# A graph attention layer on one core: Wo's tiles in PSUM, two low halves on another engine, and three steps issued sooner

## The chip, the core and the metric

The kernel runs on one core of a Trainium2 chip. A core has a matrix engine (TensorE, PE in the profile, with its weight loads as PEld), three engines that work on tiles (VectorE is DVE, ScalarE is ACT, GpSimd is POOL), and a queue that issues transfers (SyncE, SP). Each runs its own list of instructions in order; semaphores make one wait for another. Tiles lie in SBUF; TensorE adds its products up in PSUM, which this kernel uses as banks of 128 x 512 float32.

The metric is the device time of one launch, in microseconds (us). Lower is better. All times below without a unit are in us.

## What is computed

A layer norm with ReLU in front, graph attention with 16 heads of 64 and two projections one behind the other for q, k and v, and a residual sum. N is 384 rows, D is 1024 columns.

```python
h = jnp.maximum(_layernorm(x, axis=-1), 0.0)
q = h @ wq.T + bq
k = h @ wk.T + bk
v = h @ wv.T + bv
q2 = (q @ wiq.T + biq).reshape(N, H, D).transpose(1, 0, 2)
k2 = (k @ wik.T + bik).reshape(N, H, D).transpose(1, 0, 2)
v2 = (v @ wiv.T + biv).reshape(N, H, D).transpose(1, 0, 2)
mask = _build_mask(edge_index, edge_type, edge_type_weights, x.dtype)
scores = jnp.einsum('hnd,hmd->hnm', q2, k2) * scale + mask[None]
attn = jax.nn.softmax(scores, axis=-1)
out = jnp.einsum('hnm,hmd->hnd', attn, v2)
out = out.transpose(1, 0, 2).reshape(N, OUT_F)
x = x + out @ wo.T + bo
```

The mask is built from 6,528 edges: softplus of an edge type's weight where there is an edge, minus infinity elsewhere.

## The kernel before

**Weights.** Seven matrices of 1024 x 1024 are read in eight pieces (chunks) of 128 x 1024 float32, 512 KB each, in one sequence of 56: eight of Wv (0 to 7), Wq (8 to 15), Wiv (16 to 23) and Wk (24 to 31), then Wiq and Wik by turns (32 to 47: 33, 35, 37 are Wik's first, second and third), then Wo (48 to 55). `load(w)` issues the transfer of chunk w on SP's queue into one of four buffers `raw`.

**Two halves.** Every product is made from three: high x high, high x low and low x high (`mm3`, lines 494 to 496). Each chunk is therefore split. `split_hi` has ScalarE write the high half (line 102, float16 with a scale; line 108 for Wik, without one). The low half is what is left: `split_lo` (lines 125 and 127) in one instruction, `lo_half` (118) in two parts on VectorE, `lo_pieces` (113) in four parts on GpSimd.

**Slots.** Chunks 0 to 31 are taken one at a time, a slot each. `slot_head(w)` first splits chunk w + 2, finishes the products of the slot before (`flush`), sums up what the summing loads brought (`scan_sum`), then issues `load(w + 5)` and `scan_load(w)`. TensorE's 24 matmuls of the slot follow, or 18 with 512 columns for Wiv.

**Summing loads.** The weights Wiv, Wk, Wiq, Wik and Wo are read a second time, ahead of their use, for a bound on their rows that sets the float16 scale (`SCANS`, `scan_load`, line 146). ScalarE squares or takes absolute values and sums (line 155), or VectorE reduces (line 153). When all eight pieces of a matrix are there, `bound_max` (line 182) reduces them, TensorE transposes the result (line 187, `bound`), and VectorE makes scales of it (lines 162 to 201).

**Mask and residual.** GpSimd scatters the edges into a table in memory (line 351), issues three mask loads from it (360), and adds the bias bo to x in six pieces of 128 x 512 (`residual_add`, line 666) in slots 26 to 31. VectorE merges the three mask loads into the mask, a copy under a condition each (`mask_select`, line 364), in the heads of chunks 33 to 35, and scales it (744).

**Attention.** From chunk 32 on a hand-written schedule of 60 steps runs. At even steps below 48, `do_S` makes two tiles of scores (line 957, PSUM banks of tag "s", four of them). VectorE adds the mask and takes the minimum (966), ScalarE takes the exponential (971) and writes the high half of the normalised row block (1001), VectorE the low half (1005), and SP transposes both by a transfer (1009); the last two tiles go through TensorE, ScalarE and VectorE (1014, 1020, 1021). Eight attention products (`av_mm`, line 1029) follow, at steps 14, 20, 26, 32, 38, 44, 50 and 54; each is evacuated by ScalarE (1034) and split by VectorE and GpSimd (1037, 1038).

**Filling.** Between these TensorE works off a list. `fill(n)` hands out as many units as a step has left: `STEP` less what the scores and the attention product take, divided by `UNIT`. First come the products of chunks 32 to 47 (`fill_qk`, bank tag "g", three of them), whose heads (`qk_head`) hold the splits and loads for later chunks, then those of Wo (`fill_o`). A product of Wo, `omm(t, h, k)`, is three matmuls of 512 columns for one of six output tiles and one of eight chunks. All six tiles are added up in two groups: chunks 0 to 3, then a sum into the result (`ysum`, line 902), then chunks 4 to 7 in a new bank and another sum. `wo_prep` splits Wo's chunk 2 to 7 at the steps in `WSTEPS`; `wready` holds the step from which a chunk may be used. Behind the loop stand the products with the last chunk, each with its sum and its transfer to memory; the sixth tile is done in two halves of 256 columns.

`later` is a list that is worked off in the next step, behind its line 966; what is put there by an entry of it runs a step later still.

Of the kernel before, what the change touches and what calls it, by code (L numbers as in the profile page):

```python
# [19 lines left out]
N, D, NT, KT, NP = 384, 1024, 3, 8, 8  # L20
# [7 lines left out]
def gnn_kernel(ctx: ExitStack, tc: tile.TileContext, x, edges, erows, etw, wq, wk, wv, wiq, wik, wiv, wo,  # L28
# [6 lines left out]
    nc = tc.nc  # L35
# [497 lines left out]
    w = 0  # L533
# [8 lines left out]
    def slot_head(w):  # L542
        if w > 0:
            split_hi(w + 2)
        planes_of(w - 9, vT, vF, u_v)
        if w > 17:
            planes_of(w - 18, qT, qF, u_q7)
        if w != 1:
            flush()
        scan_sum(w)  # L550
        bound_max(w)
        split_lo(w + 2)
        while post:
            post.pop(0)()
        h_planes(w)
        load(w + 5)
        scan_load(w)

    def bounds(w):
# [95 lines left out]
    def residual(k):  # L655
# [5 lines left out]
        if 1 <= k < 4:  # L661
            nc.sync.dma_start(xb[k - 1], x[(k - 1) * 128:k * 128, :])

    def residual_add(i):
        y = res[:, i // 2, i % 2 * 512:i % 2 * 512 + 512]
        nc.gpsimd.tensor_tensor(y, y, bob[i % 2], OP.add)
# [37 lines left out]
    for k in range(8):  # L704
        slot_head(w)
        hi, lo = whl[w]
        for t in range(NT):
            for h in range(2):
                mm3(accs[t * 2 + h], vT[:, 0, k, t * 128:(t + 1) * 128], vT[:, 1, k, t * 128:(t + 1) * 128],
                    hi[:, h * 512:(h + 1) * 512], lo[:, h * 512:(h + 1) * 512], k == 0, k == KT - 1)  # L710
        bounds(w)
        detects(2)
        scatters(2)
        if k == 0:
            mask_base()
        w += 1

# [46 lines left out]
    def extra_k(m):  # L764
# [9 lines left out]
        if m >= 5:  # L774
            mask_load(m - 5)
        if m >= 2:
            residual_add(m - 2)
    v2_early()
# [37 lines left out]
    def qk_head(w):  # L816
# [7 lines left out]
        split_hi(w + 2, None, False, 2 if w + 2 < WO else 1)  # L824
        eng = nc.gpsimd if (w + 2) % 2 == PAR else None
        if w + 2 >= WO:
            later.append(lambda: later.append(lambda: split_lo(w + 2)))
        elif eng is None and now[0] >= 0:
# [39 lines left out]
    DT = (0,)  # L868
    PRE, STEP, UNIT, SMM, AMM = 90, 1.96, 0.168, 0.7, 1.69
    WSTEPS = (36,38,41,44,47,51)  # L870
    LD = 2
# [3 lines left out]
    oacc = {}  # L875
# [14 lines left out]
    def omm(t, h, k, c=(0, 512)):  # L890
        hi, lo = (a[:, h * 512 + c[0]:h * 512 + c[1]] for a in whl[WO + k])
        mm3(oacc[t, h][:, c[0]:c[1]], ao[:, 0, k, t * 128:(t + 1) * 128], ao[:, 1, k, t * 128:(t + 1) * 128],
            hi, lo, k in (0, KH), k in (KH - 1, KT - 1))

# [16 lines left out]
    def fill_o():  # L911


        first = [(a, k) for c in (0, 2) for a in range(3) for k in (c, c + 1)]
        first += [(a, k) for a in range(3, 6) for k in range(KH)]
        for a, k in first:
# [4 lines left out]
            omm(*OT[a], k)  # L921
            if k == KH - 1:
                ysums.append(a)
            yield 4
        bank_step = (0, 0, 0, 49, 50)
        todo = [(a, k) for k in range(KH, 7) for a in (0, 1, 3, 4, 2)]
        while todo:
# [5 lines left out]
            todo.remove(ready[0])  # L933
            if k == KH:
                oacc[OT[a]] = bank("gggss"[a])
            omm(*OT[a], k)
# [126 lines left out]
    for i in range(S + 12):  # L1063
# [4 lines left out]
        if scores:  # L1068
            do_S(i)
        fill(r / 2)  # L1070
        for o in range(2):
# [16 lines left out]
        if i in t_at:  # L1088
            turn_mm(t_at[i])
        if i in a_at:  # L1090
            av_mm(a_at[i])
# [28 lines left out]

    for a in range(5):
        omm(*OT[a], 7)
        finish(a)
    for c in ((0, 256), (256, 512)):
        oacc[OT[5]] = bank("g" if c[0] else "a")
        for k in range(KH, 8):
            omm(*OT[5], k, c)
        finish(5, c)

# [38 lines left out]
```

## Time and profile before

| What | us |
|---|---|
| Median of three runs | 278.83 |
| Fastest and slowest of them | 278.33 and 280.55 |
| The profiled execution | 279.53 |
| Its span, from the first to the last instruction | 277.4 |

The profile tells of one execution, the profiled one. Of its 279.53, 277.4 lie between the first and the last instruction. TensorE's granted clock is 1.00 throughout.

A row of the timeline reads: start, duration, engine, line, operation, the tile written and the tile read with their shapes, and how many instructions were merged. Behind it, in brackets, may stand how long the engine was idle before, and what released it. Matmuls overlap, so their drawn durations are longer than the distance between their starts. A row of the chain of waits reads: start, duration, and what the end of the program waited for at that time, followed back from the last instruction.

### The profile page before, as it was taken

To read this page: it belongs to the slowest core of one execution; us is meant where nothing else is said; L and a number is where in the kernel's file an instruction comes from. 1 tells how busy PE (TensorE), PEld (TensorE's weight loads), DVE (VectorE), ACT (ScalarE), POOL (GpSimd) and SP (SyncE) were. 2 spreads that over 40 slices of the span, in tenths; PEclk is the share of its full clock that TensorE was granted. 3 is DMA by queue.
4 is the path that set the end of the run, shared out by engine and by line. 5 is a ranking of instruction groups with operands and counts; after the bars stand their busy time and mean duration, and the time that the engine had idled before them with its cause. 6 is when DMAs were issued, how large, how long until landed. Compare 5 with 4: busy or idle time off the path is not lost.

```text
span 277.4 us, 5039 instructions
## 1 busy us (share of the span) xinstructions
PE 268.0 (97%) x1626; PEld 186.9 (67%) x1626; DVE 235.0 (85%) x565; ACT 215.1 (78%) x417; POOL 141.3 (51%) x163
## 2 busy tenths in 40 slices
PE   7899999999999999999998999999999999799995
PEld 6799999999974444666657857766666574244543
DVE  3868986999998975898999899999869899999633
ACT  3787687599896967999857488989979989888300
POOL 4665754655768565457992135565474503202310
PEclk9999999999999999999999999999999999999999
DMA  6899999999989987798999942799997989967406
GB/s 234 256 313 404 369 395 368 339 312 408 347 245 395 393 278 251 267 341 273 314 370 394 356 139 92 141 185 222 235 207 144 200 217 152 242 163 114 85 5 225
DMA packets 58090, 72.05 MB, mean 260 GB/s; under 512 B 41040, under 2 KB 42576, under 8 KB 58064
## 3 DMA queue, kind: packets, MB, share of 16 engines
q1 hardware_dynamic: 56000, 69.93, 83.3%
q0 software_dynamic: 2064, 1.80, 2.1%
q8 instruction: 13, 0.21, 0.3%
q14 instruction: 13, 0.11, 0.1%
HBM read 59.27 MB, written 3.39 MB: 226 GB/s over the span
## 4 chain that ended last, share of the span: by engine, by line
PE 76%; DVE 10%; DMA 5%; ACT 4%; issue 3%; SPq 0%; POOL 0%; DVEq 0%; ACTq 0%; POOLq 0%
PE g L494 19%; PE g L496 18%; PE g L495 18%; PE s L957 4%; PE a L1029 4%; PE s L494 3%; PE s L495 3%; PE s L496 3%; DVE whl L125 3%; DMA g<-in_wik_dram 3%; DMA g<-in_x_dram 2%; PE g L595 2%; DVE ma L364 2%; ACT e L971 1%; DVE l L153 1%
## 5 line engine op out<-in xcount | busy, mean ns | idle before, releaser
L494 PE MATMUL g<-g,whl 128*128 128x384 f32 (+1 forms) x248 | 85.1, 343 | 0.3 <-DVE iq L797 0.3
L496 PE MATMUL g<-g,whl 128*128 128x384 f32 (+1 forms) x248 | 82.6, 333 | 0.3 <-DVE whl L125 0.3
L351 POOL DMA_INDIRECT tab<-edge x51 | 61.3, 1201 | 42.0 <-DMA tab<-edge 28.7
L495 PE MATMUL g<-g,whl 128*128 128x384 f32 (+1 forms) x248 | 82.4, 332 | 0.0
L102 ACT ACTIVATE whl<-raw,small 128x1024 f16<-128x1024 f32 (+1 forms) x36 | 34.6, 971 | 3.9 <-DVE small L570 3.1
L125 DVE SCALAR_TENSOR_TENSOR whl<-raw,small,whl 128x1024 f16<-128x1024 f32 x24 | 34.3, 1430 | 4.0 <-ACT whl L102 3.7
L1005 DVE SCALAR_TENSOR_TENSOR pl<-e,s,pl 128x384 f16<-128x384 f32 x46 | 32.0, 696 | 5.9 <-ACT pl L1001 5.7
L494 PEld LDWEIGHTS g<-g,whl 128*128 128x128 f32 x184 | 34.6, 188 | 3.5 <-issue 2.8
L495 PEld LDWEIGHTS g<-g,whl 128*128 128x128 f32 x184 | 34.6, 188 | 0.0
L496 PEld LDWEIGHTS g<-g,whl 128*128 128x128 f32 x184 | 34.5, 188 | 0.0
L971 ACT ACTIVATE e<-e,s 128x384 f32<-128x384 f32 x48 | 29.1, 606 | 4.0 <-DVE s L966 3.9
L1001 ACT ACTIVATE pl<-e,s 128x384 f16<-128x384 f32 x46 | 27.7, 605 | 3.2 <-POOL s L987 3.1
L966 DVE CUSTOM_DVE_ANT_0 e<-s,ma,small 128x384 f32<-128x384 f32 x48 | 29.2, 609 | 0.4
L987 POOL TENSOR_SCALAR s<-s 128x2 f32<-128x2 f32 x23 | 8.7, 380 | 38.8 <-DVE s L985 38.8
L108 ACT ACTIVATE whl<-raw 128x1024 fp32r<-128x1024 f32 (+1 forms) x30 | 25.2, 847 | 1.1 <-DMA raw<-in_wv_dram 1.1
L155 ACT ACTIVATE g<-g 128x1024 f32<-128x1024 f32 x16 | 16.7, 1047 | 6.0 <-DMA g<-in_wik_dram 4.2
L127 DVE TENSOR_TENSOR whl<-raw,whl 128x1024 fp32r<-128x1024 f32 x15 | 19.1, 1276 | 2.4 <-ACT whl L108 2.3
L155 ACT ACTIVATE scan<-scan 128x1024 f32<-128x1024 f32 x20 | 20.9, 1044 | 0.0
L494 PE MATMUL g<-hk,whl 128*128 128x384 f16 x64 | 20.9, 326 | 0.0
L495 PE MATMUL g<-hk,whl 128*128 128x384 f16 x64 | 20.9, 326 | 0.0
L496 PE MATMUL g<-hk,whl 128*128 128x384 f16 x64 | 20.9, 326 | 0.0
L113 POOL TENSOR_TENSOR whl<-raw,whl 128x256 fp32r<-128x256 f32 x20 | 16.3, 824 | 6.9 <-ACT whl L108 5.1
(196 smaller groups left out, 553.0 us busy)
## 6 DMA issues: line engine op xcount, KB each, us to landing
raw<-in_wv_dram SPq DMA_DIRECT2D x8, 512.0 KB
raw<-in_wq_dram SPq DMA_DIRECT2D x8, 512.0 KB
scan<-in_wiv_dram SPq DMA_DIRECT2D x8, 512.0 KB
raw<-in_wiv_dram SPq DMA_DIRECT2D x8, 512.0 KB
scan<-in_wk_dram SPq DMA_DIRECT2D x8, 512.0 KB
raw<-in_wk_dram SPq DMA_DIRECT2D x8, 512.0 KB
raw<-in_wiq_dram SPq DMA_DIRECT2D x8, 512.0 KB
g<-in_wo_dram SPq DMA_DIRECT2D x8, 512.0 KB
```

What stands on the lines that cost most here:

```text
L102: soon(j if parts > 1 else -1, lambda c=c: nc.scalar.activation(hi[:, c], raw[w][:, c], AF.Copy, scale=sc))
L108: soon(j if parts > 1 else -1, lambda c=c: nc.scalar.activation(hi[:, c], raw[w][:, c], AF.Copy))
L125: nc.vector.scalar_tensor_tensor(lo, raw[w], sc, hi, op0=OP.mult, op1=OP.subtract)
L155: nc.scalar.activation(x, x, AF.Square if n in ("k", "iq", "ik") else AF.Abs, accum_out=l1[:, SROW[n], k:k + 1])
L351: nc.gpsimd.indirect_dma_start(out=tabs[c // RNG], out_offset=bass.IndirectOffsetOnAxis(ap=idx[:, c:c + 1], axis=0), in_=val[:, c:c + 1], ...
L494: nc.tensor.matmul(ps, lhi, rhi, start=first, stop=False)
L495: nc.tensor.matmul(ps, lhi, rlo, start=False, stop=False)
L496: nc.tensor.matmul(ps, llo, rhi, start=False, stop=last)
L966: nc.vector.tensor_tensor_reduce(e, st_ps.pop(i)[:, :N], ma[:, t, :], neg_c, 3.0e38, OP.add, OP.min, s[:, i % 2:i % 2 + 1])
L971: nc.scalar.activation(es[i], es[i], AF.Exp, bias=s[:, o:o + 1], scale=-1.0, accum_out=s[:, 2 + o:3 + o])
L1001: nc.scalar.activation(planes[i][:, 0, :], es[i], AF.Copy, scale=factor(i))
L1005: nc.vector.scalar_tensor_tensor(pl[:, 1, :], es.pop(i), factor(i), pl[:, 0, :], op0=OP.mult, op1=OP.subtract)
```

## The change

Nine edits in one function:

- In slots 23 to 31 the summing loads are issued ahead of the slot's weight load.
- Of the six bias additions two are made in slots 22 and 23, the others in slots 26 to 29.
- The low halves of chunks 35 and 37 (Wik's second and third) are made by VectorE in one instruction each, instead of by GpSimd.
- The low halves of Wo's chunks 0 and 1 are made one step sooner.
- Wo's chunks 2 and 3 are split at steps 35 and 37, instead of 36 and 38.
- `STEP` is 1.94, not 1.96.
- Output tiles 3, 4 and 5 stay in their PSUM bank for all eight chunks; tiles 0, 1 and 2 are still added up in two groups, with the second one of 0 and 1 in banks of tag "s" from steps 49 and 50 on. The order of the products and of the last chunk's follows from that, and tile 2 is the one done in two halves at the end.
- Within Wo's first products, all three tiles take chunk 2, then all three chunk 3.
- At steps with scores `av_mm` is called directly behind `do_S`.

```diff
@@ slot_head
-        load(w + 5)
+        if w < 23:
+            load(w + 5)
         scan_load(w)
+        if w >= 23:
+            load(w + 5)
@@ slots 16 to 23
+        if k >= 6:
+            residual_add(adds.pop(0))
@@ slots 24 to 31
-        if m >= 2:
-            residual_add(m - 2)
+        if m >= 2 and adds:
+            residual_add(adds.pop(0))
@@ qk_head
-        eng = nc.gpsimd if (w + 2) % 2 == PAR else None
+        eng = nc.gpsimd if (w + 2) % 2 == PAR and w + 2 not in (35,37,) else None
         if w + 2 >= WO:
-            later.append(lambda: later.append(lambda: split_lo(w + 2)))
+            later.append(lambda: split_lo(w + 2))
@@ constants
-    PRE, STEP, UNIT, SMM, AMM = 90, 1.96, 0.168, 0.7, 1.69
-    WSTEPS = (36,38,41,44,47,51)
+    PRE, STEP, UNIT, SMM, AMM = 90, 1.94, 0.168, 0.7, 1.69
+    WSTEPS = (35,37,41,44,47,51)
@@ omm
+        two = OT.index((t, h)) < 3
...
-            hi, lo, k in (0, KH), k in (KH - 1, KT - 1))
+            hi, lo, k == 0 or two and k == KH, two and k == KH - 1 or k == KT - 1)
@@ fill_o
-        first = [(a, k) for c in (0, 2) for a in range(3) for k in (c, c + 1)]
+        first = [(a, k) for a in range(3) for k in (0, 1)] + [(a, k) for k in (2, 3) for a in range(3)]
         first += [(a, k) for a in range(3, 6) for k in range(KH)]
...
-            if k == KH - 1:
+            if k == KH - 1 and a < 3:
                 ysums.append(a)
...
-        bank_step = (0, 0, 0, 49, 50)
-        todo = [(a, k) for k in range(KH, 7) for a in (0, 1, 3, 4, 2)]
+        bank_step = (49,50,0, 0, 0, 0)
+        todo = [(a, k) for k in range(KH, 7) for a in (3, 4, 5, 0, 1)]
...
-            if k == KH:
-                oacc[OT[a]] = bank("gggss"[a])
+            if k == KH and a < 2:
+                oacc[OT[a]] = bank("s")
@@ the schedule
         if scores:
             do_S(i)
+            if i in a_at:
+                av_mm(a_at[i])
...
-        if i in a_at:
+        if i in a_at and not scores:
             av_mm(a_at[i])
@@ the end
-    for a in range(5):
+    for a in (3, 4, 5, 0, 1):
         omm(*OT[a], 7)
         finish(a)
     for c in ((0, 256), (256, 512)):
-        oacc[OT[5]] = bank("g" if c[0] else "a")
+        oacc[OT[2]] = bank("g" if c[0] else "a")
         for k in range(KH, 8):
-            omm(*OT[5], k, c)
-        finish(5, c)
+            omm(*OT[2], k, c)
+        finish(2, c)
```

More of the change, by code (lines that the diff above doesn't have):

```diff
@@ L662, in residual @@
             nc.sync.dma_start(xb[k - 1], x[(k - 1) * 128:k * 128, :])
+    adds = list(range(6))
     def residual_add(i):
```

## The prediction

> **What bounds the kernel now.** I read the page first, then the busy time by stages, then the timeline around each idle stretch of TensorE, then the chain of waits.
>
> ```profile
> span 277.4 us, 5039 instructions
> PE 268.0 (97%) x1626; PEld 186.9 (67%) x1626; DVE 235.0 (85%) x565; ACT 215.1 (78%) x417; POOL 141.3 (51%) x163
> ...
> 149.00:162.00 13.00, 11.60 (x70) 8.44 (x69) 11.96 (x25) 7.95 (x15) 2.81 (x2) 1.00 0.78 300
> 162.00:220.00 58.00, 57.97 (x392) 38.58 (x391) 52.17 (x134) 52.69 (x123) 32.97 (x43) 1.00 0.86 182
> 220.00:240.00 20.00, 18.35 (x130) 9.95 (x129) 18.56 (x44) 17.68 (x40) 3.95 (x9) 1.00 1.01 203
> 240.00:270.00 30.00, 30.00 (x183) 13.82 (x182) 22.70 (x49) 17.36 (x35) 7.20 (x11) 1.00 0.51 99
> ```
>
> In a stage row the first pair of numbers is the stretch and its length, then busy time of TensorE, its weight loads, VectorE, ScalarE and GpSimd, then clock and DMA. TensorE is full in two of the four, and in the stages before them, so only 149–162 and 220–240 have something to give. The timeline there:
>
> ```profile
> 149.24 0.34 PE L496 MATMUL g<-g,whl 128*128 128x384 f32 x1
> 150.44 0.29 PE L187 MATMUL g<-ident,small 128*128 128x128 f32 x1 [0.86 <-DVE small L182]
> ...
> 152.07 0.32 PE L494 MATMUL g<-g,whl 128*128 128x384 f16 x1 [0.27 <-DVE iq L797]
> ...
> 161.59 0.34 PE L496 MATMUL g<-g,whl 128*128 128x384 f16 x1 [0.27 <-DVE whl L125]
> ...
> 237.65 0.39 PE L494 MATMUL g<-whl,g 128*128 128x512 f16 x1
> 239.69 0.38 PE L495 MATMUL g<-whl,g 128*128 128x512 f16 x1 [1.65 <-DVE whl L125]
> 239.91 0.38 PE L496 MATMUL g<-whl,g 128*128 128x512 f16 x1
> ```
>
> The brackets hold idle time and its releaser. Matmuls start 0.22 apart though each is drawn 0.38 long (239.69, 239.91), so a stall costs its idle time and some 0.17 more: 239.69 − 237.65 − 0.22 = 1.82. The others cost 1.03, 0.44 and 0.44. Together they are 3.73: all that this change can win, unless it shortens start or end, which it does not touch.
>
> **The first three stalls.** They lie on one chain:
>
> ```profile
> 138.26 7.19 DMA g<-in_wik_dram
> ...
> 151.13 2.58 POOL L127 TENSOR_TENSOR whl<-raw,whl 128x1024 fp32r<-128x1024 f32 x1 [4.89 <-ACT whl L108]
> 151.93 3.16 DVE L364 COPY_PREDICATED ma<-mbs 128x1152 f32<-128x1152 int32 x1
> ...
> 158.82 1.55 DVE L364 COPY_PREDICATED ma<-mbs 128x1152 f32<-128x1152 int32 x1
> ...
> 161.97 3.54 DVE L364 COPY_PREDICATED ma<-mbs 128x1152 f32<-128x1152 int32 x1
> ```
>
> The last summing load of Wik lands 7.19 after its issue; ScalarE sums it, evacuates the last k tile, and VectorE reaches the bound (L182) just before TensorE's 150.44. From there VectorE's queue carries the delay on: mask copy, score scales, second mask copy, low half of the next weight.
>
> *Summing loads sooner (slots 23 to 31).* Each 512 KB summing load is now issued ahead of the same slot's weight load. The one before this had 4.7 from issue to sum:
>
> ```profile
> 133.75 0.33 SPq L146 DMA_DIRECT2D g<-in_wik_dram  x1
> ...
> 138.49 1.06 ACT L155 ACTIVATE g<-g 128x1024 f32<-128x1024 f32 x1 [0.37 <-DMA g<-in_wik_dram]
> ...
> 141.06 0.80 POOL L360 DMA_DIRECT2D mbs<-tab  x1
> ```
>
> The load of 138.26 waits for its buffer, not for the queue, so its issue stays; what goes is one 512 KB weight load out of those ahead of it. I put it between 7.2 (nothing won) and 4.7, and take the lower part, some 2 sooner, as the previous piece is the nearest row. Weight loads now stand behind a summing load that waits for a buffer; they are used three slots of 24 matmuls later, which hides it. If that cover went, the first matmul of a slot would wait for what is missing.
>
> *Bias additions sooner.* Two of the six GpSimd additions move to slots 22 and 23, where TensorE is full and the additions fall into GpSimd's waits for scatters. The two that go stood here:
>
> ```profile
> 143.25 1.86 DVE L127 TENSOR_TENSOR whl<-raw,whl 128x1024 fp32r<-128x1024 f32 x1
> ...
> 143.89 2.34 POOL L666 TENSOR_TENSOR res<-res,bot 128x512 f32<-128x512 f32 x1
> ...
> 145.03 1.62 DVE L519 TENSOR_TENSOR g<-f,g 128x384 fp32r<-128x384 f32 x1
> ...
> 147.78 0.56 DVE L519 TENSOR_TENSOR g<-f,g 128x384 fp32r<-128x384 f32 x1 [0.46 <-ACT g L518]
> ...
> L127 DVE TENSOR_TENSOR whl<-raw,whl 128x1024 fp32r<-128x1024 f32 x15 | 19.1, 1276 | 2.4 <-ACT whl L108 2.3
> ```
>
> The same L519 takes 0.56 with GpSimd quiet and 1.62 beside it. VectorE wins 1.06 there and about 0.5 on L127, 1.6 in all. So both inputs of L182, sum and queue, come 1.6 to 2 sooner; TensorE wanted it at 149.24 + 0.17 = 149.41, 1.03 before it came. The stalls of 1.03 and 0.44 go, with half a microsecond to spare.
>
> *Wik's first low halves on VectorE.* Two subtracts (chunks 35 and 37) leave GpSimd, and VectorE gets two of 1.28 (mean of the row above; it includes some contention). Against that the mask copies at 151.93 and 161.97 lose GpSimd beside them and fall to the 1.55 of 158.82. Queue time: 3.16 becomes 1.55 + 1.28 = 2.83, and 3.54 becomes 2.83, or 0.33 and 0.71 less. The third stall's chain thus runs at least as far ahead as TensorE does (1.47 + 0.44), so 0.44 goes as well.
>
> The Trainium skill, "SBUF — State Buffer", Who interferes with whom, says that a VectorE instruction with two SBUF inputs and a GpSimd one that reads SBUF exclude each other for the whole instruction. By it the first copy ends 1.55 after GpSimd's 153.71, at 155.26; the trace has 155.09, so it agrees.
>
> **Wo's chunks.** From 221 on VectorE and ScalarE are nearly full; they start that stretch waiting for TensorE (first row), so an earlier TensorE takes them along.
>
> ```profile
> 222.27 0.58 ACT L796 ACTIVATE iq<-g,small 128x384 f16<-128x384 f32 x1 [0.70 <-PE g L496]
> ...
> 237.29 0.62 DVE L1005 SCALAR_TENSOR_TENSOR pl<-e,s,pl 128x384 f16<-128x384 f32 x1 [0.22 <-ACT pl L1001]
> ...
> 238.36 1.28 DVE L125 SCALAR_TENSOR_TENSOR whl<-raw,small,whl 128x1024 f16<-128x1024 f32 x1
> ...
> 248.74 0.74 DVE L902 SCALAR_TENSOR_TENSOR res<-g,small,res 128x512 f32<-128x512 f32 x1
> ```
>
> The stall of 1.82 is for Wo's chunk 3 (L125 at 238.36). One step sooner, its low half passes the L1005 and L966 before it and starts 1.07 sooner. The new order of `fill_o` also wants it later: three products of chunk 2, three matmuls of 0.22 each, come first instead of one, 1.3 more cover. Together 2.4 against 1.82. But what passes it also delays VectorE's rest, and the first of tiles 3 to 5 now waits for tile 0's sum to free its bank, within 0.1 of TensorE's arrival. I charge 0.2 for both (0 to 0.6).
>
> Three of the 13 sums of a PSUM tile (L902, 0.74 each) are gone. They stood in steps 45 to 48, so VectorE's last softmax work comes 2.2 sooner. TensorE issues as many matmuls as before; moving `av_mm` up in even steps moves nothing, as `fill` gives out nothing there.
>
> **The new wait.** STEP 1.94 and the products that are ready sooner push S later and put less work behind it. Between the seventh attention product and the eighth there were six Wo products and two transpositions; the built order now has four.
>
> ```profile
> 259.08 0.39 PE L494 MATMUL g<-g,g 128*128 128x512 f16 x1
> ...
> 259.19 0.58 ACT L1034 ACTIVATE aof<-a,small 128x384 f32<-128x384 f32 x1 [2.57 <-PE a L1029]
> ...
> 260.85 1.40 DVE L125 SCALAR_TENSOR_TENSOR whl<-raw,small,whl 128x1024 f16<-128x1024 f32 x1 [0.68 <-ACT whl L102]
> ...
> 262.16 0.55 DVE L1021 SCALAR_TENSOR_TENSOR pt<-s,pt 128x384 f16<-128x384 f32 x1
> ...
> 263.06 0.56 DVE L1021 SCALAR_TENSOR_TENSOR pt<-s,pt 128x384 f16<-128x384 f32 x1 [0.35 <-ACT pt L1020]
> ...
> 263.73 1.65 PE L1029 MATMUL a<-pt,vhl 128*64 128x384 f16 x18
> ```
>
> After the seventh product (its successor starts at 259.08) ScalarE evacuates it and only then splits Wo's last chunk; VectorE's low half of that stands ahead of the two L1021 for which the eighth product waits. In before this chain, 4.65, was just covered. Now the second L1021 needn't wait for its transposition and follows at once: the chain is 4.2 (259.08 to 262.16, two of 0.55). The cover falls by two products of 0.65 to 3.3. I charge 0.95 (0.4 to 1.4).
>
> **Sum.** −1.03 − 0.44 − 0.44 − 1.82 + 0.2 + 0.95 = −2.6. On the profiled execution's 279.53 (span 277.4 and 2.1 around it) that is 276.9; it lay 0.7 above the median of the runs, 278.83, from which I get **276.3**, 0.9% less.
>
> **Rivals.** *The load comes no sooner.* Between 138 and 144 GpSimd issues three mask loads (141.06 is one) into the same DMA engines; if these set the 7.19, the order on SP's queue is nothing. Then L182 stays at 150.2, two stalls remain, the third loses 0.33 of 0.44: −1.82 − 0.33 + 0.2 + 0.95 = −1.0, 277.8. For it: pieces of the same size landed in 4.7 before the mask loads began. The Trainium skill, "DMA: Bandwidth & Descriptors", Queues, rings and completion order, lets each DMA engine alternate between queues, which speaks for it. No run here shows the two apart.
>
> *Slower: VectorE is the bound from 143 to 168.* Its queue there has almost no gap. If the copies stay long for another reason than GpSimd's subtract, the two subtracts come on top, 2.56, and the sooner load is lost in that queue. It decides from a copy of 3.16 − 1.28 = 1.9.
>
> ```profile
> 167.35 0.61 DVE L966 CUSTOM_DVE_ANT_0 e<-s,ma,small 128x384 f32<-128x384 f32 x1
> ...
> 168.65 0.59 PE s L957 x6
> ```
>
> The first three stalls stay, and the third grows by 1.28; then the scores at 168.65 wait for the banks that L966 frees at 167.9: 167.9 + 2.56 is 0.5 behind 168.65 + 1.28. With VectorE late, Wo's stall stays too, and the new wait comes: +1.28 + 0.5 + 0.95 = +2.7, 281.6. Against it stands the copy of 1.55 and, in 162–220, 5.8 of VectorE's time left over.
>
> *All is won:* the eighth product is hidden after all, −3.73, 275.1.
>
> **Chances.** Forecast 0.50, load no sooner 0.20, all won 0.17, slower 0.13. A change under 1% (2.8) can hardly be told from none here. The forecast's own bounds (±0.9) put 0.18 of its 0.50 beyond 1%: faster 0.18 + 0.17 = 0.35. The slower case lies on the bound, and half of it beyond: slower 0.07, within 0.58. The range takes the forecast, all won, and the first rival with its charges at their upper ends (277.8 + 0.85): 275.0 to 278.8.
>
> **What would show it.** Right: no idle before L187 near 147.5; both first L364 near 1.55 with L127 on VectorE behind; an eighth L1029 with an idle of about 0.8 behind L1021, and none over 0.5 at Wo's chunk 3. The last summing load of Wik landing over 6 after its issue would show the first rival; copies over 1.9 the second. A stall of TensorE at another place, in slots 24 to 31 by a late weight load above all, would prove the sum incomplete.

## The result, and the profile after

| What | Before | After |
|---|---|---|
| Median of 14 runs | 278.58 | 276.62 |
| Fastest and slowest of them | 277.47, 282.12 | 275.79, 280.45 |
| The profiled execution | 279.53 | 275.86 |
| Its span | 277.4 | 273.7 |

The ratio of after to before is 0.9917, with a 95% interval from 0.9889 to 0.9945: 0.8% less, so within the 1% that counted as no change. The forecast was 276.3, with a range from 275.0 to 278.8. The ratio, and medians from here on, leave out runs more than 1.5% above the fastest of their kernel; 59 runs of the kernel before, from the experiments' sessions, have 278.57, and 19 of the changed kernel 276.64.

The page of the changed kernel gives its span, the busy times and the chain of waits by engine:

```profile
span 273.7 us, 5038 instructions
...
PE 267.6 (98%) x1626; PEld 186.9 (68%) x1626; DVE 230.5 (84%) x564; ACT 215.2 (79%) x417; POOL 136.7 (50%) x161
...
PE 94%; DMA 2%; DVE 2%; ACT 0%; issue 0%; SPq 0%
```

TensorE's busy time is that of before, but 94% of the chain now runs through it. Before, it was 76%, with 10% on VectorE and 5% on transfers. The busy time by stages, with the columns of before:

```profile
145.62:158.48 12.86, 12.85 (x77) 10.82 (x77) 11.47 (x25) 8.45 (x16) 0.00 (x0) 1.00 1.03 401
...
149.00:162.00 13.00, 12.99 (x80) 9.29 (x78) 11.96 (x24) 9.21 (x16) 0.00 (x0) 1.00 0.91 353
...
220.00:240.00 20.00, 20.00 (x134) 10.42 (x134) 18.36 (x45) 17.74 (x39) 4.17 (x8) 1.00 0.91 179
```

The last two rows are the stages that had something to give: TensorE now fills them (11.60 of 13 and 18.35 of 20 before), and VectorE is as busy in them as it was. In the first row the transfers run at 401 GB/s, which is used below.

Two rows of the kernel before, for comparison: the sum of Wik's last summing load, and the bound.

```profile
145.48 1.06 ACT L155 ACTIVATE g<-g 128x1024 f32<-128x1024 f32 x1 [3.20 <-DMA g<-in_wik_dram]
...
150.15 0.15 DVE L182 TENSOR_REDUCE small<-l 128x1 f32<-128x8 f32 x1
```

The changed kernel's timeline at the places that the prediction named follows. Its line numbers have moved: L671 is L666 of before (a bias addition), L1022, L1028 and L1029 are L1014, L1020 and L1021 (the last two row blocks, through TensorE, ScalarE and VectorE), and L1037 is L1029 (an attention product). From here on, L1029 is VectorE's low half.

```profile
127.70 1.29 POOL L671 TENSOR_TENSOR res<-res,bot 128x512 f32<-128x512 f32 x1
127.72 1.31 DVE L201 TENSOR_SCALAR small<-bc,small 128x8 f32<-128x8 f32 x1
...
137.09 0.33 SPq L146 DMA_DIRECT2D g<-in_wik_dram  x1
...
143.66 1.06 ACT L155 ACTIVATE g<-g 128x1024 f32<-128x1024 f32 x1 [1.61 <-DMA g<-in_wik_dram]
...
145.96 0.56 DVE L519 TENSOR_TENSOR g<-f,g 128x384 fp32r<-128x384 f32 x1 [1.54 <-ACT g L518]
...
148.33 0.15 DVE L182 TENSOR_REDUCE small<-l 128x1 f32<-128x8 f32 x1
...
148.73 0.34 PE L496 MATMUL g<-g,whl 128*128 128x384 f32 x1
148.91 0.27 PE L187 MATMUL g<-ident,small 128*128 128x128 f32 x1
...
150.12 1.51 DVE L364 COPY_PREDICATED ma<-mbs 128x1152 f32<-128x1152 int32 x1
151.52 1.20 DVE L127 TENSOR_TENSOR whl<-raw,whl 128x1024 fp32r<-128x1024 f32 x1
...
159.62 1.54 DVE L364 COPY_PREDICATED ma<-mbs 128x1152 f32<-128x1152 int32 x1
...
234.57 1.28 DVE L125 SCALAR_TENSOR_TENSOR whl<-raw,small,whl 128x1024 f16<-128x1024 f32 x1
...
236.10 0.38 PE L495 MATMUL g<-whl,g 128*128 128x512 f16 x1
...
254.61 1.65 PE L1037 MATMUL a<-pt,vhl 128*64 128x384 f16 x18
256.19 0.39 PE L494 MATMUL s<-g,g 128*128 128x512 f16 x1
...
259.28 1.01 DVE L1029 SCALAR_TENSOR_TENSOR pt<-s,pt 128x384 f16<-128x384 f32 x2
259.54 2.09 PE L1037 MATMUL a<-pt,vhl 128*64 128x384 f16 x18
261.57 0.39 PE L494 MATMUL g<-g,g 128*128 128x512 f16 x1
```

L187 follows its predecessor by 0.18, without idle time. The first and the third mask copy, which the prediction named, take 1.5 each. Wo's chunk 3 is ready at 235.85 and wanted at 236.10. The one new wait is hidden inside the eighth attention product: it takes 261.57 − 259.54 = 2.03 where the seventh took 256.19 − 254.61 = 1.58, so 0.45 of it is waiting for L1029, which ends at 260.29.

The two profiled executions differ by 3.67, but the medians only by 2.0. Of the 3.67, 0.51 was there at TensorE's first product of the projections (11.26 before, 10.75 after) and is no work of the change. Why the rest of the difference is not all in the medians is what the experiments are about.

### The profile page after: what moved, and what is told of

Read it like the earlier page. It is cut to its first block, busy times and chain, and to the rows that moved or that the text cites. A ratio compares the mean times of both kernels' runs of the same rounds, so it can differ in the third digit from the quotient of the medians.

```text
span 273.7 us, 5038 instructions
## 1 busy us (share of the span) xinstructions
PE 267.6 (98%) x1626; PEld 186.9 (68%) x1626; DVE 230.5 (84%) x564; ACT 215.2 (79%) x417; POOL 136.7 (50%) x161
## 4 chain that ended last, share of the span: by engine, by line
PE 94%; DMA 2%; DVE 2%; ACT 0%; issue 0%; SPq 0%
PE g L494 24%; PE g L496 23%; PE g L495 23%; PE s L965 5%; PE a L1037 5%; PE s L494 3%; PE s L496 3%; PE s L495 3%; DMA g<-in_x_dram 2%; PE g L598 2%; PE a L495 1%; PE a L494 1%; PE a L496 1%; DVE whl L125 1%; DVE lnt L374 0%; ACT whl L102 0%
## 5 line engine op out<-in xcount | busy, mean ns | idle before, releaser
L1013 DVE SCALAR_TENSOR_TENSOR pl<-e,s,pl 128x384 f16<-128x384 f32 x46 | 31.4, 683 | 7.0 <-ACT pl L1009 7.0
L125 DVE SCALAR_TENSOR_TENSOR whl<-raw,small,whl 128x1024 f16<-128x1024 f32 x24 | 32.8, 1368 | 4.6 <-ACT whl L102 3.6
L127 DVE TENSOR_TENSOR whl<-raw,whl 128x1024 fp32r<-128x1024 f32 x17 | 21.0, 1237 | 2.4 <-ACT whl L108 2.1
L113 POOL TENSOR_TENSOR whl<-raw,whl 128x256 fp32r<-128x256 f32 x20 | 17.0, 858 | 9.3 <-issue 6.2
L809 POOL TENSOR_TENSOR ik<-f,ik 128x384 f16<-128x384 f32 x7 | 6.4, 913 | 28.2 <-DVE ik L808 23.6
```

The source lines that it names most:

```text
L125: nc.vector.scalar_tensor_tensor(lo, raw[w], sc, hi, op0=OP.mult, op1=OP.subtract)
L127: (eng or nc.vector).tensor_tensor(lo, raw[w], hi.bitcast(F32), OP.subtract)
L1013: nc.vector.scalar_tensor_tensor(pl[:, 1, :], es.pop(i), factor(i), pl[:, 0, :], op0=OP.mult, op1=OP.subtract)
```

## The experiments

Unless it says otherwise, each kernel is the changed one with one part undone or altered.

**The order of the loads, by itself.**

```diff
@@ slot_head
-        if w < 23:
-            load(w + 5)
+        load(w + 5)
         scan_load(w)
-        if w >= 23:
-            load(w + 5)
```

> The changed kernel with one part undone: in slots 23 to 31 the weight load is issued ahead of the summing load again. Theory (the order on the queue decides): the last summing load of Wik takes 7.2 from issue to sum again instead of 6.57, so its sum starts 0.6 later, L182 with it, near 148.9 instead of 148.33 (both counted against TensorE's start, which varies by 0.5). TensorE reaches L187 at 148.91, 0.4 behind the end of L182, so a stall of 0.2 to 0.4 appears at L187; the time is 0.2 to 0.5 above the changed kernel's 276.6, some 276.9. Rival (the mask loads set the landing): the sum comes at the same distance from its issue as in the changed kernel, no stall, 276.6. Rival (the order is worth the whole of the forecast's 2): the sum comes 2 later, a stall of 1.5 at L187, 278.1 or more.

Median 275.91, ratio to before 0.9897 (0.986 to 0.9934). In its timeline the load is issued and summed here:

```profile
136.41 0.33 SPq L146 DMA_DIRECT2D g<-in_wik_dram  x1
...
143.26 1.06 ACT L155 ACTIVATE g<-g 128x1024 f32<-128x1024 f32 x1 [0.94 <-DMA g<-in_wik_dram]
```

By "issue to sum" is meant the time from the start of the load's issue to the start of ScalarE's sum. It is 6.85 here, there is no stall, and nothing is lost, where 0.2 to 0.5 was expected. This speaks for the first rival; the kernels with the mask loads put behind, further down, decide it.

**The bias additions in slots 26 to 31 again.**

```diff
@@ slots 16 to 23
-        if k >= 6:
-            residual_add(adds.pop(0))
```

> The changed kernel with one part undone: the six bias additions stand in slots 26 to 31 again. Theory (two engines beside each other stretch VectorE's instructions): L125 beside the addition takes 3.05 again instead of 1.27, L127 1.86 instead of 1.21 and L519 1.62 instead of 0.55, so the buffer of the last summing load is freed 1.2 later and VectorE reaches L182 some 1.8 later, near 150.1; TensorE waits 1.2 to 1.4 at L187 and 0.3 to 0.44 for the bound behind it; time 1.4 to 1.8 above the changed kernel, 278.0 to 278.4. Rival (the additions only fill GpSimd's own waits): L182 within 0.3 of the changed kernel's, no stall, 276.6.

Median 276.97, ratio 0.9935 (0.9893 to 0.9978). Its VectorE and TensorE:

```profile
128.31 3.05 DVE L125 SCALAR_TENSOR_TENSOR whl<-raw,small,whl 128x1024 f16<-128x1024 f32 x1
...
149.14 0.34 PE L496 MATMUL g<-g,whl 128*128 128x384 f32 x1
149.98 0.29 PE L187 MATMUL g<-ident,small 128*128 128x128 f32 x1 [0.50 <-DVE small L182]
```

L125 is at 3.05 again, 1.27 in the changed kernel, and the summing load goes out at 138.17 instead of 137.09, as expected. The stall is 0.67, with 0.45 behind it, and not 1.2 to 1.4. But the next kernel, which differs from the changed one only behind L187, shows the same stall, so it can't be put down to the additions.

**The low halves of chunks 35 and 37 on GpSimd again.**

```diff
@@ qk_head
-        eng = nc.gpsimd if (w + 2) % 2 == PAR and w + 2 not in (35,37,) else None
+        eng = nc.gpsimd if (w + 2) % 2 == PAR else None
```

> The changed kernel with one part undone: the low halves of chunks 35 and 37 are made by GpSimd again. Theory (the copy waits for GpSimd's subtract, so the subtract costs VectorE more there than in its own queue): the first and third L364 take 3.0 to 3.5 instead of 1.51 and 1.54, and the two L127 of 1.2 leave VectorE; its queue is 0.3 later at the first L162 and 0.7 later at the end. TensorE had about 0.5 in hand there, so the time is 0 to 0.4 above the changed kernel, 276.6 to 277.0. Rival (the copies are long for another reason): both stay at 1.5 and the queue is 1.2 shorter twice, time the same, 276.6. A time below the changed kernel's by over 0.5 would speak against both.

Median 277.07, ratio 0.9938 (0.9905 to 0.997). VectorE and GpSimd in its timeline:

```profile
151.24 1.51 DVE L364 COPY_PREDICATED ma<-mbs 128x1152 f32<-128x1152 int32 x1
...
151.80 3.12 POOL L127 TENSOR_TENSOR whl<-raw,whl 128x1024 fp32r<-128x1024 f32 x1 [9.64 <-ACT whl L108]
...
153.41 1.53 DVE L579 SCALAR_TENSOR_TENSOR small<-small 128x1 f32<-128x1 f32 x1
...
161.03 3.53 DVE L364 COPY_PREDICATED ma<-mbs 128x1152 f32<-128x1152 int32 x1
```

The first copy began before GpSimd's subtract and kept its 1.51; the subtract took 3.12 (2.58 in the kernel before), and a VectorE instruction on 128 single elements, 0.14 in the changed kernel, took 1.53 and ended with the subtract (153.41 + 1.53 = 154.94, 151.80 + 3.12 = 154.92). The copy that began behind a subtract took 3.53. So in both pairs the cost went to what started second, and the low half on GpSimd cost VectorE 1.4 to 2 either way. Not every pair is like this: in the kernel with the additions late, L125 began at 128.31, 0.68 ahead of a GpSimd addition that took its usual 1.28, and it was L125 that took 3.05; a scatter of GpSimd's was running when it began. TensorE lost 0.19 at 160.5.

The medians of these three kernels can't be told from the changed kernel's 276.64: the differences are −0.7 (−1.2 to 0.6), 0.3 (−0.4 to 1.9) and 0.4 (−0.2 to 1.0), by drawing again from the runs of both.

**Wo's chunks late again.**

```diff
@@ qk_head
-            later.append(lambda: split_lo(w + 2))
+            later.append(lambda: later.append(lambda: split_lo(w + 2)))
@@ constants
-    WSTEPS = (35,37,41,44,47,51)
+    WSTEPS = (36,38,41,44,47,51)
@@ fill_o
-        first = [(a, k) for a in range(3) for k in (0, 1)] + [(a, k) for k in (2, 3) for a in range(3)]
+        first = [(a, k) for c in (0, 2) for a in range(3) for k in (c, c + 1)]
```

> The changed kernel with one part undone: Wo's chunks 2 and 3 are split at steps 36 and 38 again, the low halves of its chunks 0 and 1 come a step later, and the first products take the old order (tile 2's chunk 2 and 3 last); STEP and the tiles in PSUM stay as changed. Theory (the stall in front of Wo's chunk 3 is a matter of when VectorE gets to its low half): in the changed kernel that half ended 0.3 ahead of TensorE; now it comes about 1.1 later and is wanted 1.3 sooner, so TensorE waits 1.6 to 2.1 there, time 1.5 to 2.1 above the changed kernel, 278.1 to 278.7. Rival (the stall is moved, not removed: what TensorE waits for there it makes up at the eighth attention product, which waited 0.45 inside): 1.1 to 1.6 above, 277.7 to 278.2.

Median 278.56, which is 1.9 above the changed kernel (1.1 to 2.5, by drawing again from the runs of both); ratio 0.9978 (0.9944 to 1.0012), so nearly the whole gain is gone. Its timeline:

```profile
234.81 0.39 PE L494 MATMUL g<-whl,g 128*128 128x512 f16 x1
236.84 0.38 PE L495 MATMUL g<-whl,g 128*128 128x512 f16 x1 [1.64 <-DVE whl L125]
...
260.21 0.56 DVE L1029 SCALAR_TENSOR_TENSOR pt<-s,pt 128x384 f16<-128x384 f32 x1 [1.00 <-ACT pt L1028]
260.88 1.65 PE L1037 MATMUL a<-pt,vhl 128*64 128x384 f16 x18
262.46 0.39 PE L494 MATMUL g<-g,g 128*128 128x512 f16 x1
```

The stall is back at its old size, 236.84 − 234.81 − 0.22 = 1.81. The eighth product takes 1.58, for seven products of Wo now stand between it and the seventh, where the changed kernel has four. In this trace the stall thus costs 1.81 − 0.45 = 1.36, which is the rival's mechanism, while the median is in the theory's range; the interval holds both. Which of the three parts undone here brings the stall back wasn't tried.

**All three parts ahead of the attention undone** (the first three diffs together).

> The changed kernel with all three parts ahead of the attention undone together: loads in the old order, all six bias additions in slots 26 to 31, the low halves of chunks 35 and 37 on GpSimd. Theory (these parts remove the stalls of 1.03, 0.44 and 0.44, but executions of the changed kernel have some of them too, as those of the two runs with one part undone had 0.67 and 0.45): the profile shows stalls at L187 and behind it of 1 to 1.5 and one of up to 0.44 at 161; the median of the times is 0.8 to 1.9 above the changed kernel's 276.6, 277.4 to 278.5. Rival (the stalls come and go with the landing of scatters and loads, whatever these parts do): median within 0.4 of 276.6. Rival (the parts cover for each other): undoing all costs over 1.9, since each alone cost 0 to 0.7.

Median 277.18, 0.5 above the changed kernel (0.1 to 2.0); ratio 0.9952 (0.9908 to 0.9997). Its profile has stalls of 1.32 and 0.44 at and behind L187 and of 0.44 at 160.5. So in one execution the three parts look worth 2.2, and in the median 0.5.

**All six tiles in two groups again** (`omm`, `bank_step`, `todo`, the banks and the last chunk as before; the first products and `STEP` as changed).

> The changed kernel with the tiles undone: all six output tiles are added up in two groups again, with the old banks, order and last chunk; the steps of Wo's chunks 2 and 3, the order of the first products up to chunk 3 and STEP stay as changed. Theory (the tiles in PSUM win nothing of their own: VectorE has three sums of 0.74 less, beside a TensorE that doesn't wait): no new stall of TensorE after 220, the eighth product waits as in the changed kernel (0.45, for its cover is the same), time within 0.4 of the changed kernel, 276.2 to 277.0. Rival (VectorE is short of time behind 236): the three sums push its queue 2.2 later in steps 45 to 50, TensorE waits 0.5 to 2 there for a bank or a split, 277.1 to 278.6.

Median 277.07, ratio 0.998 (0.9934 to 1.0025). Nine runs can't tell 0.4 from nothing, and there is no profile of it that can be set beside the others, so whether the tiles in PSUM win anything of their own stays open.

**All bias additions in slots 18 to 23.**

```diff
@@ slots 16 to 23
-        if k >= 6:
+        if k >= 2:
             residual_add(adds.pop(0))
```

> The changed kernel with all six bias additions in slots 18 to 23 instead of two in 22 and 23 and four in 26 to 29. Theory (an addition beside VectorE's L125, L127 and L519 stretches them, and where it falls changes from one execution to the next with the landing of the scatters; the last summing load of Wik is issued behind VectorE's L153): no instruction of these three lines is stretched between 128 and 145, the load's issue comes at 136 to 136.5, its sum at 142 to 143, L182 at 146 to 147.5, no stall at L187 in any execution; the median falls to between 275.7 and 276.3, against 276.6. Rival (the landing of the summing load sets it, and VectorE's stretching is beside the point): issue to sum stays between 5.6 and 7.8 and the sum between 143 and 145, median within 0.3 of 276.6. Rival (the additions put the scatters off, so the mask loads and the first copy come late): the first L364 waits for its load, 277 or more.

Median 277.72 from five runs, ratio 0.9966 (0.9913 to 1.002): no gain. The theory failed and its last rival came true. The additions put GpSimd's scatters off, so the first mask load went out at 143.31, and the first copy (L364, at 152.14) waited 1.30 for it. No L125 was stretched any more, yet the summing load went out at 137.88, later than in the changed kernel: the L153 ahead of it now waited 1.64 for a summing load of Wo. It was summed 6.42 after its issue. Stalls of 0.69, 0.43, 0.32 and 0.91 stand between 149 and 161.5.

**The eighth product's chain sooner.**

```diff
@@ constants
-    WSTEPS = (35,37,41,44,47,51)
+    WSTEPS = (35,37,41,44,47,50)
@@ the loop over the steps
+        if i in t_at:
+            turn_mm(t_at[i])
         fill(r / 2)
...
-        if i in t_at:
-            turn_mm(t_at[i])
```

> The changed kernel with two steps of the eighth attention product's chain sooner: Wo's last chunk is split at step 50 instead of 51, ahead of ScalarE's evacuation of the seventh product, and TensorE transposes the two last row blocks ahead of the products of their step instead of behind them. Theory (the eighth product waits for VectorE's low half of that chunk and the two L1029 behind it, 0.45 inside): the product takes 1.58 to 1.65 from its start to the next matmul instead of 2.03, the time falls by 0.4 to 0.5 in each execution, median 276.1 to 276.3. Rival (the wait is not for that chain): 2.03 stays, 276.6. Rival (the transposition now waits for GpSimd's normalisation, which ends at 256.4, 0.2 behind the seventh product): a stall of 0.2 to 0.5 at L1022 takes it back, 276.4 to 276.7.

Median 277.0, ratio 0.9968 (0.9923 to 1.0012); the gain of 0.2 is below what the runs can tell. The timeline shows it:

```profile
260.00 0.49 PE L1022 MATMUL s<-ident,e 128*128 128x128 f32 x3
...
261.05 0.56 DVE L1029 SCALAR_TENSOR_TENSOR pt<-s,pt 128x384 f16<-128x384 f32 x1 [1.51 <-ACT pt L1028]
261.06 1.89 PE L1037 MATMUL a<-pt,vhl 128*64 128x384 f16 x18
262.89 0.39 PE L494 MATMUL g<-g,g 128*128 128x512 f16 x1
```

The product takes 1.83, so 0.25 of waiting is left: the second transposition belongs to step 52 and still stands behind step 51's products, at 260.00, and the last L1029 waits 1.51 for what follows it.

The same profile has a stall of 1.27 at L187, although not one instruction ahead of it differs from the changed kernel's. Four profiles of the same code up to L187 had by now given stalls of none, 0.67, none and 1.27. What differed between them was the last summing load of Wik, so the last four kernels went for that load.

**The changed kernel once more.**

> The changed kernel itself, once more, beside the three that follow. Theory (its executions differ in when the last summing load of Wik lands, and that in when the three mask loads were issued beside it): L182 comes 4.67 behind the start of that load's sum, as in all ten profiles so far; issue to sum lies between 5.6 (mask loads issued 3.7 or more after it) and 8.6 (first one before it); where it is over 7 a stall of 0.6 to 1.3 stands at L187; median 276.3 to 276.9. Rival (the profiled execution without a stall is what the change always gives): no stall, issue to sum near 6.6.

Median 276.76, ratio 0.9899 (0.9848 to 0.9951). The profiled execution has the stall, as the theory expected:

```profile
137.08 0.33 SPq L146 DMA_DIRECT2D g<-in_wik_dram  x1
...
144.12 1.06 ACT L155 ACTIVATE g<-g 128x1024 f32<-128x1024 f32 x1 [2.00 <-DMA g<-in_wik_dram]
...
148.06 0.34 PE L496 MATMUL g<-g,whl 128*128 128x384 f32 x1
148.79 0.15 DVE L182 TENSOR_REDUCE small<-l 128x1 f32<-128x8 f32 x1
...
149.09 0.29 PE L187 MATMUL g<-ident,small 128*128 128x128 f32 x1 [0.69 <-DVE small L182]
```

It is the same kernel as that of the result's trace, with 7.04 from issue to sum instead of 6.57, and 0.86 of stall (149.09 − 148.06 − 0.17) instead of none. The first of the three mask loads went out at 136.32, 0.76 ahead of the summing load.

**The mask loads behind the summing load.**

```diff
@@ mask_load
-        nc.gpsimd.dma_start(mbt[g], ...)
+        nc.sync.dma_start(mbt[g], ...)
@@ slots 24 to 31
-        if m >= 5:
-            mask_load(m - 5)
+        if m == 6:
+            for g in range(3):
+                mask_load(g)
```

> The changed kernel with the three mask loads moved from GpSimd's queue to SP's, behind the last summing load of Wik and the weight load of slot 30. Theory (the mask loads, 576 KB each, share the DMA engines with that load and hold it up by some 1.4 each): issue to sum falls to 4.7 to 5.8, sum near 142.3, L182 near 147, no stall at L187 and none behind it in any execution; the median is 0.4 to 0.8 below the changed kernel's of the same call. Rival (mask loads don't matter, the landing is late for what stands ahead on SP's own queue): issue to sum stays at 6.5 to 8, median within 0.3. Rival (the masks now come too late): the first L364, at 148.7, waits for its load, TensorE stalls by 0.5 to 2 at or behind L187, median 0.3 to 1.5 above.

Median 275.85, ratio to before 0.9874 (0.9826 to 0.9922), the lowest of all kernels, though the old load order by itself had 275.91. Its timeline:

```profile
135.78 0.42 SPq L80 DMA_DIRECT2D raw<-in_wiq_dram  x1
137.87 0.33 SPq L146 DMA_DIRECT2D g<-in_wik_dram  x1
...
141.25 2.36 SPq L360 DMA_DIRECT2D mbs<-tab  x3
...
143.04 1.06 ACT L155 ACTIVATE g<-g 128x1024 f32<-128x1024 f32 x1
...
147.71 0.15 DVE L182 TENSOR_REDUCE small<-l 128x1 f32<-128x8 f32 x1
```

Issue to sum is 5.17, against 7.04 in the changed kernel of the same session. TensorE comes to L187 at 149.07 without a stall, and the first copy, at 149.50, doesn't wait for its load.

**The same with the loads in the old order** (the first diff on top).

> The kernel before this with the loads in the old order: in slots 23 to 31 the weight load goes ahead of the summing load. Theory (the order itself is worth one 512 KB transfer, 1.2 to 1.3: of two profiles with the first mask load at the same 140.30, the one in the new order had 5.62 from issue to sum and the one in the old order 6.85): issue to sum is 1.2 to 1.3 longer than in the kernel before this; L182 near 148.2, 0.5 ahead of TensorE's need, so the time is the same within 0.3. Rival (the order is nothing): issue to sum within 0.4 of the kernel before this.

Median 275.9, ratio 0.9874 (0.9826 to 0.9921).

```profile
135.42 0.33 SPq L80 DMA_DIRECT2D raw<-in_wik_dram  x1
137.68 0.33 SPq L146 DMA_DIRECT2D g<-in_wik_dram  x1
...
142.85 1.06 ACT L155 ACTIVATE g<-g 128x1024 f32<-128x1024 f32 x1
```

Again 5.17: the order is nothing. The L80 rows say why. Every slot issues one weight load and one summing load, and all of them were swapped. The weight load of the same slot no longer stands ahead of the summing load, but that of the slot before, which was itself put behind, now does. Both rows show one 512 KB weight load some 2 us ahead.

All twelve runs of these two kernels are at or below 276.60; of the changed kernel's 19, ten are above. Their median is 0.8 below it (0.2 to 1.1, by drawing again); against the changed kernel's six runs of the same session it is 0.9 (−0.1 to 1.3).

**Mask loads behind, and the eighth product sooner** (both diffs).

> The changed kernel with the mask loads behind the last summing load, and with the eighth attention product's chain sooner (Wo's last chunk split at step 50, the two transpositions ahead of their step's products). Theory (two separate gains): no stall at L187, and the eighth product 0.2 shorter than with a cover as changed; median 0.6 to 1.0 below the changed kernel's of the same call, 275.5 to 276.0. Rival (an earlier TensorE runs into VectorE at Wo's chunk 3, where the changed kernel had 0.3 in hand): 0.3 to 0.8 of it comes back as a stall in front of chunk 3.

Median 276.29, ratio 0.989 (0.984 to 0.9939): no better than with the mask loads alone. In the profiled execution TensorE lost 0.77 at 120, the load went out only at 138.42 and was summed 6.25 later, and L187 stalled by 0.51. No stall stands in front of Wo's chunk 3, so the rival didn't come. The eighth product again took 1.82.

The profiles side by side. "Scores" is the start of TensorE's first six score matmuls; "attention" is from there to the start of the matmul behind the eighth product.

| Kernel | Load issued | First mask load | Issue to sum | Sum to L182 | Scores | Attention |
|---|---|---|---|---|---|---|
| before | 138.26 | 138.08 | 7.22 | 4.67 | 160.23 | 105.08 |
| changed | 137.09 | 136.90 | 6.57 | 4.67 | 158.41 | 103.16 |
| changed, again | 137.08 | 136.32 | 7.04 | 4.67 | 158.87 | 103.16 |
| old load order | 136.41 | 140.30 | 6.85 | 4.67 | 158.26 | 103.16 |
| additions late | 138.17 | 137.98 | 6.84 | 4.67 | 159.76 | 103.14 |
| low halves on GpSimd | 136.98 | 137.26 | 7.80 | 4.67 | 159.53 | 103.35 |
| Wo late | 136.60 | 140.30 | 5.62 | 4.67 | 157.94 | 104.52 |
| all three undone | 136.97 | 135.58 | 7.99 | 4.67 | 159.71 | 103.59 |
| additions early | 137.88 | 143.31 | 6.42 | 4.67 | 159.44 | 104.05 |
| eighth product sooner | 136.54 | 135.71 | 8.59 | 4.67 | 159.90 | 102.99 |
| masks behind | 137.87 | 141.25 | 5.17 | 4.67 | 158.42 | 103.15 |
| masks behind, old order | 137.68 | 140.53 | 5.17 | 4.67 | 158.33 | 103.16 |
| masks behind, eighth sooner | 138.42 | 141.69 | 6.25 | 4.67 | 159.43 | 103.00 |

Three things stand in it. The attention takes the same time to 0.02 in six of the seven profiles whose code is the same there; the seventh, with the additions early, has 0.9 more, which is its stall of 0.91 at 161. The time up to the scores ranges from 157.94 to 159.90 over five profiles whose code up to L187 is the same (changed, again, low halves, Wo late, eighth sooner). And L182 follows the sum by 4.67 every time.

Issue to sum also holds the wait for what stands ahead on SP's queue. Five of these traces record when both that weight load and the summing load landed, counted from each issue:

| Kernel | Weight load ahead: issued, to landing | Summing load: issued, to landing | Landed behind it by |
|---|---|---|---|
| changed, again | 135.23, 5.8 | 137.08, 7.0 | 3.0 |
| additions early | 136.04, 7.1 | 137.88, 6.4 | 1.1 |
| masks behind | 135.78, 6.0 | 137.87, 5.1 | 1.2 |
| masks behind, old order | 135.42, 6.1 | 137.68, 5.1 | 1.3 |
| masks behind, eighth sooner | 136.56, 6.8 | 138.42, 6.2 | 1.3 |

In the first row a mask load had been issued ahead of the summing load on GpSimd's queue, in the other four none had, and there the summing load landed 1.1 to 1.3 behind the weight load ahead instead of 3.0.

## Why the prediction was right, and where it was wrong

**What there was to win** held: apart from the start, the profiled executions differ by the four stalls and the wait in the eighth product, and by 0.1 beside them.

**"What goes is one 512 KB weight load out of those ahead of it … some 2 sooner"** failed. Another weight load takes the place of the one removed, and the two orders gave 5.17 and 5.17. The first rival had the better mechanism: the mask loads hold the landing up, by some 1.8 in the one trace of the table of landings that has one ahead (3.0 against 1.1 to 1.3). Issue to sum is 6.57 to 8.59, 7.4 on average, in the seven rows in which the first mask load goes out ahead of the summing load or within 0.3 of it, and 5.17 to 6.85, 5.9 on average, in the six in which it goes out 2.8 or more behind. Within the six, 6.42 and 6.25 are no work of the mask loads: there the weight load ahead landed 5.3 and 4.9 after the summing load's issue, against 3.9 in the two with 5.17. For 6.85 and 5.62 the traces hold no landings, and their difference isn't settled. At the 401 GB/s that the transfers reached from 145.62 to 158.48 in the changed kernel, a mask load of 576 KB is 1.5 long.

The Trainium skill, "DMA: Bandwidth & Descriptors", Queues, rings and completion order, has each DMA engine take turns between the queues it has work for. The runs agree: issued ahead of it on GpSimd's own queue, the mask load held up a load of SP's queue, which landed 3.0 behind its predecessor; issued behind it on the same queue, the mask loads did not, with 1.2 and 1.3.

**"Both inputs of L182, sum and queue, come 1.6 to 2 sooner"** was wrong about the queue, though not in its number: in the two profiled executions L182 comes 1.82 sooner (150.15 and 148.33). But 1.17 of this is the load's issue, which the forecast held fixed, and only 0.65 the shorter way from issue to sum (7.22 and 6.57), which it had at some 2. VectorE stood idle for 1.54 ahead of L519 in the changed kernel, waiting for ScalarE's L518, which stands behind the sum in ScalarE's own order. What L182 needs is the sum, but it stands in VectorE's list behind L519 and two more; so 4.67 follows the sum's start each time, whatever GpSimd does beside it. The additions act further ahead: a stretched L125 delays L153, which frees the buffer into which the summing load goes. That made its issue 1.2 later before (138.26 against 137.09) and 1.1 with the additions late. This has no fixed price either: with all three parts undone the additions stand in the same slots, but that L125 took 1.27 and the issue came at 136.97; with all additions early it came at 137.88, as told above. How far it reaches TensorE is decided by the landing.

So **the first two stalls, 1.03 and 0.44**, were charged as gone, but they come and go with that landing, in both kernels. The changed kernel's profiled execution escaped by 0.28: where L187 waits it follows L182's start by 0.30 (148.79 and 149.09 in the second profile), and 148.33 + 0.30 lies that much ahead of 148.91. Before's profiled execution was a late one, 0.96 above its median, and after's an early one, 0.78 below. The attention is 1.92 shorter than in before's profile in each profile that has its code; the medians differ by 1.9 to 2.0, and the ratio's 0.8% is 2.3. That leaves 0 to 0.4 for these two stalls, where the forecast had 1.47; with the whole interval of the ratio, 1.5 to 3.1, it is anything from −0.4 to 1.2. This is worked out on the assumption that before's attention, of which there is one profile, is as steady.

**The low halves** held: copies of 1.51 and 1.54 (forecast 1.55), and the third stall gone. It returned with 0.19 and 0.44 where the subtracts went back to GpSimd. The second rival, copies that stay long, fell. The Trainium skill, "SBUF — State Buffer", Who interferes with whom, says of the ports that VectorE shares with GpSimd: "Issue order, not op shape, decides who blocks." The copy of 1.51 beside a subtract of 3.12, and the copy of 3.53 behind one, agree. The L125 of 3.05, which began ahead of the addition beside it, doesn't fit this by itself.

**Wo's stall** held: 1.82 gone, and 1.81 back when its timing was undone. The lead over that kernel is 1.81 + 0.25 = 2.1, where the forecast had 2.4. The charge of 0.2 for what waits behind did not show; the attention is 0.1 shorter than stalls and wait add up to (−1.82 − 0.43 + 0.45 = −1.80, against −1.92).

**The new wait** was right in mechanism and mis-sized: 0.45, not 0.95. The chain took 260.29 − 256.19 = 4.10 (forecast 4.2) and the cover was 259.54 − 256.19 = 3.35 (forecast 3.3). But the product needs the low planes that L1029 makes only from its fifth matmul on (`av_mm` takes the term with them last, one head and then the other): in the trace five of its matmuls start from 259.54 to 259.89, and the sixth, for the second head, at 260.34.

**The sum.** −2.6 was forecast, −2.0 came. By the medians, the two stalls that were mostly not won (1.1 to 1.5 too much) were offset in part by the wait (0.5 too much charged), by the charge of 0.2 that did not show and by the 0.1 that the attention is shorter beside. That the forecast came so near is the luck of this compensation; what was right in it is Wo's stall and the third one. The third rival, that all is won, is nearest to the profiled execution alone: 3.67 less, of which 0.51 is the start's.

## What to carry to other kernels

A stall that hangs on a transfer has no fixed price: take the same stretch from two or three executions before a single profile's idle time goes into a sum, and split the span at a point that such a wait can't reach, as the attention here, to see what a change does in every execution. When an order of issue is swapped in every step, write the new list out to the end: what was taken away in one step comes back from its neighbour. And where one late transfer decides, put other transfers that aren't needed yet behind it on the same queue; here that gave 275.9, below both kernels, with all twelve runs within 1.4, where the old load order alone came to the same median with runs from 275.24 to 277.42.

## What the runs showed of the hardware

A VectorE instruction on 128 single elements took 1.53 instead of 0.14 beside a GpSimd subtract, and both ended together: the price isn't set by its own size. The same is in the changed kernel's timeline at 127.70, where a small L201 took 1.31 instead of 0.23 and ended with a GpSimd addition (127.72 + 1.31 = 129.03, 127.70 + 1.29 = 128.99).

Two loads of 512 KB issued some 2 us apart on one queue landed 1.1 to 1.3 apart, and 3.0 apart in the one trace where a load of 576 KB had been issued on another queue between them.
